# Graph attention with residual and layer norm: softmax rows replaced by the row's largest entry, with the general path behind a branch

## The chip, the cores and the metric

The kernel runs on one core of one Trainium2 chip; the other cores are idle. The metric is device time in microseconds (us) of one execution of the whole program. The span is the time from the first to the last instruction of the profiled execution.

## What is computed

x is 4096 x 512, adj is 4096 x 4096, W is 512 x 2048 (four heads of 512 columns), a is 4 x 1024 x 1, all float32. The reference, cut to what matters:

```python
ht = (h @ W).reshape(N, 4, 512).transpose(1, 0, 2)
src = einsum('hnd,hd->hn', ht, a[:, :512, 0])
dst = einsum('hnd,hd->hn', ht, a[:, 512:, 0])
e = leaky_relu(src[:, :, None] + dst[:, None, :], 0.01) + adj[None]
att = softmax(e, axis=-1)
h_prime = einsum('hij,hjd->hid', att, ht).mean(axis=0)
x = layernorm(x + h_prime)
```

adj is zero but for some 70,000 entries, each drawn evenly between 0.05 and 1e9, and its diagonal is never zero. So the largest entry of a row of adj can stand far above every other number in that row's softmax.

## The kernel before, in words

The scores src and dst are made first (lines 61 to 118): a is copied to all partitions (L68), W and x are loaded (L73, L75), DVE multiplies W by a (L83), and PE transposes x (L94) and multiplies (L101, L107, L111). x and W stay on chip. Then comes the attention, in 128 units: a block of 128 rows of adj by one of four heads. For each of the eight chunks of 512 columns of a unit, `add` makes the score (ACT L153, DVE L154) and adds adj with the row's maximum (DVE L156), `exp` takes the exponential with its sum (ACT L168), `transpose` turns the chunk on PE in four pieces (L173) and copies it out of PSUM (ACT L176 or DVE L178), and `apply` multiplies it by x, four matmuls of 128 x 512 (PE L186). `scale`, `turn` and `project` divide by the sum (DVE L197), transpose again (PE L202, ACT L204) and multiply by W (PE L211). After a block's fourth head come residual and norm (DVE L217 to L231), and POOL issues the store (L232).

The loop at L244 sets the order: the chunks of one unit are in the matrix products while the next unit's scores are made and the one before it is projected. SP issues the loads of adj in pieces of 128 x 1024 (L134), the next block's as soon as the last head has read a piece.

## Time and profile before

| | us |
|---|---|
| three timed runs | 4704.34, 4705.52, 4705.82 |
| median | 4705.52 |
| span of the profiled execution | 4702.5 |
| median less span (launch and end, around the span) | 3.0 |
| PE busy with matmuls | 4596.1 |
| DVE busy | 2124.3 |
| ACT busy | 1811.9 |
| POOL busy | 18.2 |

The profiled execution's own time isn't recorded apart from its span; what lies around the span is taken to be the 3.0 us by which the median exceeds it. PE is the engine whose busy time nearly fills the span. In the profile a group of instructions is told by its line, engine and operation, what it writes and reads, its count, its busy time and the mean of one in ns, and then the idle time ahead of it and what ended that. The granted clock (PEclk) is 1.00 at TensorE's higher level of 2.4 GHz and 0.50 at its lower level of 1.2 GHz.

### The profile page before, as it was taken

How to read it: one execution, taken by the hardware profiler on the slowest of the kernel's cores; microseconds unless marked ns; L12 is line 12 of the kernel's file. 1: busy time of each engine (PE TensorE's matmuls, PEld its weight loads, DVE VectorE, ACT ScalarE, POOL GpSimd, SP SyncE). 2: the span in 40 equal slices, each digit the busy share in tenths (PEclk: the TensorE clock that was granted, in tenths of full speed). 3: DMA queues.
4: the chain of work that ended last, by engine and by line, in shares of the span. 5: the costliest groups of instructions: out<-in, count | busy, mean ns of one | idle time of the engine just before them, and what ended most of it. 6: DMA issues, size and time to landing. Idle time of an engine off the chain costs nothing.

```text
span 4702.5 us, 38848 instructions
## 1 busy us (share of the span) xinstructions
PE 4596.1 (98%) x14112; PEld 2251.0 (48%) x14112; DVE 2124.3 (45%) x4656; ACT 1811.9 (39%) x3712; POOL 18.2 (0%) x38
## 2 busy tenths in 40 slices
PE   7899999999999999999999999999999999999999
PEld 3344444444444444444444444444444444444444
DVE  3444444444444444444444444444444444444443
...
GB/s 125 27 12 21 18 21 20 12 12 21 18 21 20 7 16 21 18 21 16 7 21 21 18 21 16 7 21 21 18 21 12 12 21 21 18 21 12 12 21 3
DMA packets 26127, 92.66 MB, mean 20 GB/s; under 512 B 2768, under 2 KB 2768, under 8 KB 25296
## 3 DMA queue, kind: packets, MB, share of 16 engines
q1 hardware_dynamic: 22656, 75.51, 4.7%
q0 software_dynamic: 2560, 8.39, 0.5%
...
q8 instruction: 111, 1.82, 0.2%
q14 instruction: 80, 0.66, 0.0%
HBM read 81.79 MB, written 8.39 MB: 19 GB/s over the span
## 4 chain that ended last, share of the span: by engine, by line
issue 75%; PE 23%; DVE 1%; POOL 0%; DMA 0%; ACT 0%; POOLq 0%; ACTq 0%; DVEq 0%
PE y_ps L186 16%; PE o_ps L211 2%; PE pt_ps L173 2%; PE ps_b L107 1%; PE ps_sd L101 1%; PE ps_x L94 0%; DVE y L197 0%; DVE prod L83 0%; PE yt_ps L202 0%; POOL out_dram L232 0%; DMA w_sb<-in_L_gnn_W_dram 0%; DVE s L154 0%; DVE sd L103 0%; DVE s L156 0%; PE ps_s L111 0%
## 5 line engine op out<-in xcount | busy, mean ns | idle before, releaser
L186 PE MATMUL y_ps<-x_sb,pt 128*128 128x512 f32 x8192 | 3685.7, 593 | 0.0
L186 PEld LDWEIGHTS y_ps<-x_sb,pt 128*128 128x128 f32 x8192 | 1487.1, 190 | 1531.3 <-issue 1530.9
L154 DVE SCALAR_TENSOR_TENSOR s<-s 128x512 f32<-128x512 f32 x1024 | 705.6, 689 | 1048.4 <-ACT s L153 1006.2
L153 ACT ACTIVATE s<-dst_b,src 128x512 f32<-128x512 f32 x1024 | 723.0, 718 | 971.2 <-PE pt_ps L173 952.2
L178 DVE COPY pt<-pt_ps 128x512 f32<-128x512 f32 x640 | 442.6, 692 | 997.4 <-PE pt_ps L173 997.4
L168 ACT ACTIVATE s<-s,nm 128x512 f32<-128x512 f32 x1024 | 724.0, 708 | 181.0 <-DVE nm L164 181.0
L173 PEld LDWEIGHTS pt_ps<-ident,s 128*128 128x128 f32 x4096 | 512.5, 141 | 551.7 <-issue 538.7
L176 ACT COPY pt<-pt_ps 128x512 f32<-128x512 f32 x384 | 225.1, 586 | 1346.4 <-PE pt_ps L173 1346.4
L156 DVE CUSTOM_DVE_ANT_0 s<-s,adj 128x512 f32<-128x512 f32 x1024 | 708.6, 692 | 35.1
L173 PE MATMUL pt_ps<-ident,s 128*128 128x128 f32 x4096 | 615.3, 273 | 12.7 <-ACT s L168 12.7
L211 PE MATMUL o_ps<-w_sb,yt 128*128 128x512 f32 x1024 | 460.8, 593 | 0.7 <-ACT yt L204 0.7
L211 PEld LDWEIGHTS o_ps<-w_sb,yt 128*128 128x128 f32 x1024 | 184.6, 190 | 184.6 <-issue 183.6
L197 DVE TENSOR_SCALAR y<-y_ps,rz 128x512 f32<-128x512 f32 x128 | 96.0, 750 | 296.8 <-PE y_ps L186 296.8
L168 ACT ACTIVATION_READ_ACCUMULATOR s<-s,nm 128x1 f32 x1024 | 191.2, 187 | 0.0
L202 PE MATMUL yt_ps<-ident,y 128*128 128x128 f32 x512 | 83.9, 286 | 52.6 <-DVE y L197 52.6
L204 ACT COPY yt<-yt_ps 128x512 f32<-128x512 f32 x128 | 75.0, 586 | 76.0 <-PE yt_ps L202 76.0
L202 PEld LDWEIGHTS yt_ps<-ident,y 128*128 128x128 f32 x512 | 53.6, 140 | 83.5 <-DVE y L197 83.5
L224 ACT ACTIVATE sd<-sd 128x1 f32<-128x1 f32 x32 | 6.5, 203 | 210.8 <-DVE sd L223 210.8
L156 DVE DVE_READ_ACCUMULATOR2_ANT m<- 128x1 f32 x1024 | 83.8, 82 | 0.0
L217 DVE TENSOR_TENSOR y<-o_ps,x_sb 128x512 f32<-128x512 f32 x32 | 22.1, 692 | 90.2 <-PE o_ps L211 90.2
L94 PE MATMUL ps_x<-ident,x_sb 128*128 128x128 f32 x128 | 29.9, 422 | 21.8 <-DMA x_sb<-in_x_dram 16.6
L95 ACT COPY xT<-ps_x 128x512 f32<-128x512 f32 x32 | 18.7, 586 | 76.8 <-PE ps_x L94 76.8
...
## 6 DMA issues: line engine op xcount, KB each, us to landing
adj<-in_adj_dram SPq DMA_DIRECT2D x128, 512.0 KB, 3.4
x_sb<-in_x_dram SPq DMA_DIRECT2D x8, 1024.0 KB, 17.9
out_dram<-y POOLq DMA_DIRECT2D x32, 256.0 KB, 2.3
w_sb<-in_L_gnn_W_dram ACTq DMA_DIRECT2D x4, 1024.0 KB, 10.7
...
```

The costliest lines, as they stand in the source:

```text
L153: nc.scalar.activation(s, dst_b[:, h, ts(c, C)], AF.Identity, bias=src[:, ib, h : h + 1])
L154: nc.vector.scalar_tensor_tensor(s, s, SLOPE, s, op0=OP.mult, op1=OP.max)
L156: nc.vector.tensor_tensor_reduce(out=s, in0=s, in1=adj_t[ib, k][:, ts(part, C)], scale=1.0, scalar=LOWEST, op0=OP.add, op1=OP.max, accum_o ...
L168: nc.scalar.activation(s, s, AF.Exp, bias=self.nm, accum_out=self.z[:, c : c + 1])
L173: nc.tensor.transpose(ps[:, q, :], self.s[c][:, ts(q, P)], ident)
L176: nc.scalar.copy(pt, ps)
L178: nc.vector.tensor_copy(pt, ps)
L186: nc.tensor.matmul(self.y_ps, pt[:, q, :], x_sb[:, c * Q + q, :], start=(c == 0 and q == 0), stop=(c == NCH - 1 and q == Q - 1),)
L197: nc.vector.tensor_scalar_mul(self.y, self.y_ps, self.rz)
L202: nc.tensor.transpose(ps[:, kb, :], self.y[:, ts(kb, P)], ident)
L204: nc.scalar.copy(self.yt, ps)
L211: nc.tensor.matmul(o_ps[ib], self.yt[:, kb, :], w_sb[:, kb, ts(h, D)], start=(h == 0 and kb == 0), stop=(h == H - 1 and kb == KB - 1),)
```

## The change

The kernel becomes two functions. `leading_rows` handles every row by the place of its largest entry of adj; `general` is the old computation, put behind a branch, and done for those of 32 blocks that have a row in which the largest entry does not lead by enough. Blocks are now strided: block ib holds the rows p * 32 + ib, so the 128 rows of one load of adj lie 32 rows (512 KiB) apart.

For each block of adj, loaded as 128 x 4096 in a ring of six buffers, DVE takes the maximum of each stretch of 64 columns (`segment_maxima`), then the largest eight of the 64 maxima and their places (`find_segment`). POOL adds the row's offset and gathers the leading 64 columns of each row from DRAM by an indirect DMA (`lead`, 256 bytes a row). Two blocks later DVE finds the place within them (`find_column`), and POOL gathers the row of x at that place (`y`, 2 KB a row). For the last block the place is found in the whole row (`find_column_in_row`). PE transposes y (`turn`), adds x through an identity matmul (`residual`) and multiplies by `w_sum`, the mean of the four heads' W (`products`). ACT makes sums and sums of squares (`stats`) and the squared norms of x (`row_norm`); POOL makes the reciprocal deviation (`rstd`), and ACT writes the result into `hold` (`finish`), over the block of x that came in there. Before that, the last 16 blocks of `hold` hold W. Results of blocks 0 to 23 leave by six stores of four blocks each, those of 24 to 31 one block at a time, all after the last load on SP's queue but for block 31's, which ACT issues (`store`). `test` counts the rows whose lead is too small, from the two largest values, a bound on the scores (`bound`, from the norms of x and of W a) and the rounding of float32; every engine then loads the total and branches.

The main part of the diff; `block`, inside `general`, is the code of the old units, with blocks strided and its own loads and stores:

```diff
-    units = [(ib, h) for ib in range(NB) for h in range(H)]
-    before = None
-    for n in range(len(units) + 1):
...
+    leading_rows(tc, x, adj, W, a, out, ident, v, n_bad, any_bad)
+    flag = nc.values_load(any_bad[0:1, 0:1], min_val=0, max_val=N)
+    with tc.If(flag > 0, preferred_fallthrough_block=False):
+        general(tc, x, adj, W, out, ident, v, n_bad)
...
+    AHEAD = 5
+    Q = 4
+    PIECES = 4
+    LATE = NB - Q
+    adj_pool = ctx.enter_context(tc.tile_pool(name="adj_pool", bufs=AHEAD + 1))
+    small = ctx.enter_context(tc.tile_pool(name="small", bufs=5))
+    rows = ctx.enter_context(tc.tile_pool(name="rows", bufs=2))
+    psum = ctx.enter_context(tc.tile_pool(name="psum", bufs=4, space=bass.MemoryType.PSUM))
+    adj_rows = adj.rearrange("(p nb) m -> nb p m", nb=NB)
+    adj_segs = adj.rearrange("n (s e) -> (n s) e", e=E)
+    x_rows = x.rearrange("(p nb) d -> p nb d", nb=NB)
+    out_rows = out.rearrange("(p nb) d -> p nb d", nb=NB)
+    w_blocks = W.rearrange("(kb p) (h d) -> p kb h d", p=P, h=H)
+    hold = once.tile([P, NB, D], F32, name="hold")
+    w_at = NB - KB * H
...
+    def pieces(ib):
+        return PIECES if ib in (0, LATE, NB - 1) else 2 if ib > LATE else 1
+    def load_adj(ib):
+        if 0 <= ib < NB:
+            t = adj_t[ib] = adj_pool.tile([P, N], F32, name="adj_t")
+            n = pieces(ib)
+            for k in range(n):
+                nc.sync.dma_start(t[:, ts(k, N // n)], adj_rows[ib][:, ts(k, N // n)])
+    def load_x(lo, n):
+        nc.sync.dma_start(hold[:, ds(lo, n), :], x_rows[:, ds(lo, n), :])
+    def load_w(kb):
+        nc.sync.dma_start(hold[:, ds(w_at + kb * H, H), :], w_blocks[:, kb])
+    load_adj(0)
+    for s in range(2):
+        nc.scalar.dma_start(a_rows[ts(s, H), :], a[:, ts(s, D), :].rearrange("h d o -> h (d o)"))
+    for kb in range(KB):
+        load_w(kb)
+        load_adj(kb + 1)
+    load_x(0, Q)
+    for ib in range(KB + 1, AHEAD):
+        load_adj(ib)
...
+    def segment_maxima(ib, lo, hi):
+        if lo == 0:
+            seg_of[ib] = small.tile([P, S], F32, name="seg")
+        n = max(pieces(ib), 2)
+        for k in range(lo * n // PIECES, hi * n // PIECES):
+            nc.vector.tensor_reduce(
+                seg_of[ib][:, ts(k, S // n)],
+                adj_t[ib][:, ts(k, N // n)].rearrange("p (s e) -> p s e", e=E), axis=AX.X, op=OP.max,
+            )
+    def find_segment(ib):
+        seg = seg_of.pop(ib)
+        nc.vector.max(out=top[:, ib, :], in_=seg)
+        at = small.tile([P, 8], U32, name="at")
+        nc.vector.max_index(at, top[:, ib, :], seg)
+        row = small.tile([P, 1], U32, name="row")
+        nc.gpsimd.tensor_tensor(row, at[:, 0:1], first[:, ib : ib + 1], op=OP.add)
+        lead = small.tile([P, E], F32, name="lead", bufs=2 * Q + 1)
+        nc.gpsimd.indirect_dma_start(
+            out=lead, out_offset=None, in_=adj_segs,
+            in_offset=bass.IndirectOffsetOnAxis(ap=row[:, :1], axis=0),
+        )
+        start = at_of[ib] = small.tile([P, 1], U32, name="start")
+        nc.gpsimd.tensor_tensor(start, at[:, 0:1], width, op=OP.mult)
+        lead_of[ib] = lead
+    def gather_rows(ib, col):
+        y = y_t[ib] = rows.tile([P, D], F32, name="y", bufs=4)
+        nc.gpsimd.indirect_dma_start(
+            out=y, out_offset=None, in_=x,
+            in_offset=bass.IndirectOffsetOnAxis(ap=col[:, :1], axis=0),
+        )
+    def find_inner(ib):
+        nc.vector.max(out=inner[:, ib, :], in_=lead_of[ib])
+    def find_column(ib):
+        if ib < LATE - Q:
+            find_inner(ib)
+        within = small.tile([P, 8], U32, name="within")
+        nc.vector.max_index(within, top[:, ib, :], lead_of[ib])
+        col = small.tile([P, 1], U32, name="col")
+        nc.gpsimd.tensor_tensor(col, at_of.pop(ib), within[:, 0:1], op=OP.add)
+        gather_rows(ib, col)
+    def find_column_in_row(ib):
+        col = small.tile([P, 8], U32, name="col")
+        nc.vector.max_index(col, top[:, ib, :], adj_t[ib])
+        gather_rows(ib, col)
+    def turn(ib):
+        y = y_t.pop(ib)
+        tp = psum.tile([P, KB, P], F32, name="tp", bufs=2)
+        for kb in range(KB):
+            nc.tensor.transpose(tp[:, kb, :], y[:, ts(kb, P)], ident)
+        yt = yt_of[ib] = rows.tile([P, KB, P], F32, name="yt")
+        nc.scalar.copy(yt, tp)
+    def residual(ib):
+        o_ps[ib] = psum.tile([P, D], F32, name="o")
+        nc.tensor.matmul(o_ps[ib], ident, hold[:, ib, :], start=True, stop=False)
+    def products(ib, lo=0, hi=KB):
+        start = ib not in o_ps
+        if start:
+            o_ps[ib] = psum.tile([P, D], F32, name="o")
+        for kb in range(lo, hi):
+            nc.tensor.matmul(
+                o_ps[ib], yt_of[ib][:, kb, :], w_sum[:, kb, :],
+                start=(start and kb == 0), stop=(kb == KB - 1),
+            )
+    def row_norm(ib):
+        sq = rows.tile([P, D], F32, name="sq")
+        nc.scalar.activation(sq, hold[:, ib, :], AF.Square, accum_out=xx[:, ib : ib + 1])
+    def stats(ib):
+        o, i = o_ps[ib], slice(ib, ib + 1)
+        sq = rows.tile([P, D], F32, name="sq")
+        nc.scalar.activation(sq, o, AF.Identity, scale=-1.0 / D, accum_out=nm[:, i])
+        sq = rows.tile([P, D], F32, name="sq")
+        nc.scalar.activation(sq, o, AF.Square, bias=nm[:, i], accum_out=sd[:, i])
+    def rstd(i):
+        nc.gpsimd.tensor_scalar(sd[:, i], sd[:, i], 1.0 / D, EPS, op0=OP.mult, op1=OP.add)
+        nc.gpsimd.tensor_tensor(sd[:, i], sd[:, i], power[:, : i.stop - i.start], op=OP.pow)
+        nc.gpsimd.tensor_mul(nm[:, i], nm[:, i], sd[:, i])
+    def finish(ib):
+        i = slice(ib, ib + 1)
+        nc.scalar.activation(hold[:, ib, :], o_ps.pop(ib), AF.Identity, bias=nm[:, i], scale=sd[:, i])
+    def finish_last(ib, residual):
+        o = o_ps.pop(ib)
+        if residual:
+            nc.vector.tensor_add(hold[:, ib, :], o, hold[:, ib, :])
+            o = hold[:, ib, :]
+        st = small.tile([P, nc.vector.BN_STATS_DIM], F32, name="st", bufs=2)
+        nc.vector.bn_stats(st, o)
+        mv = small.tile([P, nc.vector.BN_AGGR_DIM], F32, name="mv", bufs=2)
+        nc.vector.bn_aggr(mv, st)
+        r = small.tile([P, 1], F32, name="r", bufs=2)
+        nc.scalar.activation(r, mv[:, 1:2], AF.Sqrt, bias=eps)
+        nc.vector.reciprocal(r, r)
+        nc.vector.tensor_scalar(hold[:, ib, :], o, mv[:, 0:1], r, op0=OP.subtract, op1=OP.mult)
+    def store(queue, lo, n):
+        queue.dma_start(out_rows[:, ds(lo, n), :], hold[:, ds(lo, n), :])
+    def mean_of_heads(kb):
+        o = psum.tile([P, D], F32, name="o")
+        for h in range(H):
+            nc.tensor.matmul(o, ident, hold[:, w_at + kb * H + h, :], start=(h == 0), stop=(h == H - 1))
+        nc.scalar.activation(w_sum[:, kb, :], o, AF.Copy, scale=1.0 / H)
...
+    def turn_w(kb, h):
+        tp = psum.tile([P, KB, P], F32, name="tp", bufs=2)
+        for k in range(KB):
+            nc.tensor.transpose(tp[:, k, :], hold[:, w_at + kb * H + h, ts(k, P)], ident)
+        wt = rows.tile([P, KB, P], F32, name="wt")
+        nc.scalar.copy(wt, tp)
+        return wt
+    def head_vector(kb, h, wt):
+        for k in range(KB):
+            nc.tensor.matmul(
+                pv[:, kb, h : 2 * H : H], wt[:, k, :], at_d[:, k, h : 2 * H : H],
+                start=(k == 0), stop=(k == KB - 1),
+            )
...
+    def test():
+        a1 = top[:, :, 0]
+        nc.vector.tensor_tensor(gap, top[:, :, 1], inner[:, :, 1], op=OP.max)
+        size = once.tile([P, NB], F32, name="size")
+        nc.vector.scalar_tensor_tensor(size, a1, -1.0, a1, op0=OP.mult, op1=OP.max)
+        nc.vector.tensor_sub(gap, a1, gap)
+        nc.vector.tensor_scalar(size, size, -(2.0 ** -22), lead_by, op0=OP.mult, op1=OP.subtract)
+        nc.vector.scalar_tensor_tensor(gap, gap, 0.9999, size, op0=OP.mult, op1=OP.add)
+        nc.vector.tensor_scalar(gap, gap, 0.0, None, op0=OP.is_gt)
...
+    x_at = {lo - 1: (lo, Q) for lo in range(Q, LATE - Q, Q)}
+    x_at.update({ib - 2: (ib, 1) for ib in range(LATE - Q, LATE)})
+    vectors = [(kb, h) for kb in range(KB) for h in range(H)]
+    vectors_at = {t: 2 if t < 3 else 1 for t in range(1, 15)}
+    COLUMN, PROJECT, STATS, FINISH = 2, 3, 4, 6
+    for t in range(NB):
+        if t in x_at:
+            load_x(*x_at[t])
+        load_adj(t + AHEAD)
+        middle = 1 if t == NB - 1 else 2
+        segment_maxima(t, 0, middle)
+        if t >= COLUMN:
+            find_column(t - COLUMN)
+        segment_maxima(t, middle, PIECES)
+        pair = t >= FINISH and t % 2 == 0
+        if pair:
+            rstd(slice(t - FINISH, t - FINISH + 2))
+        find_segment(t)
+        if t < 2:
+            mean_of_heads(t)
+        elif t == 2:
+            mean_of_heads(2)
+            mean_of_heads(3)
+        if t == 0:
+            turn_a()
+        turned = [(*vectors[0], turn_w(*vectors.pop(0))) for _ in range(vectors_at.get(t, 0))]
+        if t == 16:
+            head_norms()
+        ib = t - PROJECT
+        if ib >= 0:
+            turn(ib)
+            if ib < LATE:
+                residual(ib)
+        for some in turned:
+            head_vector(*some)
+        if ib >= 0:
+            products(ib)
+        if t >= STATS:
+            stats(t - STATS)
+            row_norm(t - STATS)
+        if pair:
+            finish(t - FINISH)
+            finish(t - FINISH + 1)
+    load_x(LATE, NB - LATE)
+    for lo in range(0, NB - 2 * Q, Q):
+        store(nc.sync, lo, Q)
+    for ib in range(NB - 2 * Q, NB - FINISH):
+        store(nc.sync, ib, 1)
+    find_column(NB - 2)
+    rstd(slice(NB - FINISH, NB - FINISH + 2))
+    find_column_in_row(NB - 1)
+    for ib in range(LATE, NB):
+        row_norm(ib)
+    turn(NB - 3)
+    bound(0)
+    products(NB - 3, 0, KB - 1)
+    finish(NB - FINISH)
+    finish(NB - FINISH + 1)
+    turn(NB - 2)
+    products(NB - 3, KB - 1, KB)
+    bound(1)
+    bound(2)
+    finish_last(NB - 4, True)
+    for ib in range(LATE - Q, NB):
+        find_inner(ib)
+    test()
+    products(NB - 2, 0, KB - 1)
+    finish_last(NB - 3, True)
+    turn(NB - 1)
+    products(NB - 2, KB - 1, KB)
+    for ib in (NB - FINISH, NB - FINISH + 1):
+        store(nc.sync, ib, 1)
+    residual(NB - 1)
+    products(NB - 1, 0, KB - 1)
+    pg = count()
+    products(NB - 1, KB - 1, KB)
+    for ib in (NB - 4, NB - 3):
+        store(nc.sync, ib, 1)
+    finish_last(NB - 2, True)
+    store(nc.sync, NB - 2, 1)
+    report(pg)
+    finish_last(NB - 1, False)
+    store(nc.scalar, NB - 1, 1)
...
+    with tc.For_i(0, NB, 1) as ib:
+        here = nc.values_load(n_bad[0:1, ds(ib, 1)], min_val=0, max_val=P)
+        with tc.If(here > 0):
+            block(ib)
```

How the instructions stand on the engines. DVE before, some of the steady order of a unit (s is a chunk of scores, m its maxima, pt a transposed chunk):

```order
L178 COPY pt<-pt_ps 128x512
L154 SCALAR_TENSOR_TENSOR s<-s 128x512
L156 ISA s,m<-s,adj_552 128x512
L156 ISA m 128x1
L154 SCALAR_TENSOR_TENSOR s<-s 128x512
L156 ISA s,m<-s,adj_554 128x512
L156 ISA m 128x1
```

DVE in the change, two half blocks in the steady part (seg holds the 64 maxima, top the largest eight):

```order
L164 MAX_INDEX at<-top,seg 128x8
L155 TENSOR_REDUCE seg<-adj_t 128x32
L184 MAX inner<-lead 128x8
L191 MAX_INDEX within<-top,lead 128x8
L155 TENSOR_REDUCE seg<-adj_t 128x32
L162 MAX top<-seg 128x8
L164 MAX_INDEX at<-top,seg 128x8
L155 TENSOR_REDUCE seg<-adj_t 128x32
```

What was chunk work on scores is now one pass over adj, with four short searches in each block.

SP before, its first rows:

```order
L296 UNCONDITIONAL_BRANCH
L75 DMA x_sb<-in_x_dram 128x4x512 x8
L134 DMA adj_550<-in_adj_dram 128x1024
L134 DMA adj_552<-in_adj_dram 128x1024
L134 DMA adj_554<-in_adj_dram 128x1024
L134 DMA adj_556<-in_adj_dram 128x1024
```

SP in the change, the last loads and what stands behind them:

```order
L113 DMA hold<-in_x_dram 128x512
L110 DMA adj_t<-in_adj_dram 128x2048 x2
L113 DMA hold<-in_x_dram 128x512
L110 DMA adj_t<-in_adj_dram 128x2048 x2
L110 DMA adj_t<-in_adj_dram 128x1024 x4
L113 DMA hold<-in_x_dram 128x2048
L260 DMA out_dram<-hold 128x2048 x6
L260 DMA out_dram<-hold 128x512 x7
L60 TENSOR_LOAD any_bad
L60 ISA x2
```

Every store but that of block 31 stands behind every load on SP's queue.

POOL before issued only 32 stores. In the change, one block with `rstd` and the next one's start:

```order
L178 DMA y<-in_x_dram,col 128x512
L166 TENSOR_TENSOR row<-at,first 128x1
L168 DMA lead<-in_adj_dram,row 128x64
L173 TENSOR_TENSOR start<-at,width 128x1
L193 TENSOR_TENSOR col<-start,within 128x1
L178 DMA y<-in_x_dram,col 128x512
L236 TENSOR_SCALAR sd<-sd 128x2
L237 TENSOR_TENSOR sd<-sd,power 128x2
L238 TENSOR_TENSOR nm<-nm,sd 128x2
```

Each block has two gathers on POOL, and `rstd`, which waits for ACT's `stats`, stands between a gather of y and the next gather of lead.

## Rows read from the trace of the kernel before

**Rows 1.** The page: span, busy time and share of each engine, GB/s by slices.
```profile
span 4702.5 us, 38848 instructions
...
PE 4596.1 (98%) x14112; PEld 2251.0 (48%) x14112; DVE 2124.3 (45%) x4656; ACT 1811.9 (39%) x3712; POOL 18.2 (0%) x38
...
GB/s 125 27 12 21 18 21 20 12 12 21 18 21 20 7 16 21 18 21 16 7 21 21 18 21 16 7 21 21 18 21 12 12 21 21 18 21 12 12 21 3
```

**Rows 2.** The page: the chain that ended last, shares by engine.
```profile
issue 75%; PE 23%; DVE 1%; POOL 0%; DMA 0%; ACT 0%; POOLq 0%; ACTq 0%; DVEq 0%
```

**Rows 3.** Groups by line, PE: busy, mean ns | idle before, releaser.
```profile
L186 PE MATMUL y_ps<-x_sb,pt 128*128 128x512 f32 x8192 | 3685.7, 593 | 0.0
...
L173 PE MATMUL pt_ps<-ident,s 128*128 128x128 f32 x4096 | 615.3, 273 | 12.7 <-ACT s L168 12.7
...
L211 PE MATMUL o_ps<-w_sb,yt 128*128 128x512 f32 x1024 | 460.8, 593 | 0.7 <-ACT yt L204 0.7
```

**Rows 4.** The chain in order of time: start us, us, what (two blocks).
```profile
1156.29 141.36 issue
1298.20 141.35 issue
```

**Rows 5.** Windows of the start: busy PE, PEld, DVE, ACT, POOL; PEclk, DMA share, GB/s.
```profile
2.00:12.00 10.00, 0.00 (x0) 0.00 (x0) 0.00 (x0) 0.00 (x0) 0.00 (x0) 1.00 0.97 388
12.00:22.00 10.00, 1.94 (x8) 1.57 (x8) 8.63 (x25) 0.18 (x1) 0.00 (x0) 1.00 1.02 405
22.00:32.00 10.00, 7.86 (x30) 4.49 (x30) 9.55 (x28) 5.70 (x9) 0.00 (x0) 1.00 1.04 395
32.00:36.00 4.00, 0.00 (x0) 0.00 (x0) 3.79 (x11) 0.00 (x0) 0.00 (x0) 0.84 1.05 385
40.00:50.00 10.00, 10.00 (x28) 5.62 (x26) 2.85 (x5) 1.62 (x3) 0.00 (x0) 0.50 0.00 0
```

**Rows 6.** DMA queues: packets, MB, share; issues by line: KB each, us to landing.
```profile
q1 hardware_dynamic: 22656, 75.51, 4.7%
q0 software_dynamic: 2560, 8.39, 0.5%
...
x_sb<-in_x_dram SPq DMA_DIRECT2D x8, 1024.0 KB, 17.9
out_dram<-y POOLq DMA_DIRECT2D x32, 256.0 KB, 2.3
w_sb<-in_L_gnn_W_dram ACTq DMA_DIRECT2D x4, 1024.0 KB, 10.7
```

**Rows 7.** Groups by line, DVE.
```profile
L154 DVE SCALAR_TENSOR_TENSOR s<-s 128x512 f32<-128x512 f32 x1024 | 705.6, 689 | 1048.4 <-ACT s L153 1006.2
...
L164 DVE TENSOR_REDUCE nm<-m 128x1 f32<-128x8 f32 x128 | 20.6, 161 | 4.5
```

**Rows 8.** Groups by line, ACT.
```profile
L168 ACT ACTIVATE s<-s,nm 128x512 f32<-128x512 f32 x1024 | 724.0, 708 | 181.0 <-DVE nm L164 181.0
...
L168 ACT ACTIVATION_READ_ACCUMULATOR s<-s,nm 128x1 f32 x1024 | 191.2, 187 | 0.0
...
L204 ACT COPY yt<-yt_ps 128x512 f32<-128x512 f32 x128 | 75.0, 586 | 76.0 <-PE yt_ps L202 76.0
```

**Rows 9.** Timeline, PE at the lower granted clock (39 to 50 us).
```profile
39.10 7.19 PE L107 MATMUL ps_b<-sd,ident 8*128 8x512 f32 x8 [0.77 <-DVE sd L103]
...
46.55 3.82 PE L94 MATMUL ps_x<-ident,x_sb 128*128 128x128 f32 x16
```

**Rows 10.** Groups by line, POOL: the store that POOL issues.
```profile
L232 POOL DMA_DIRECT2D out_dram<-y x32 | 17.5, 546 | 4679.8 <-DVE y L231 4679.8
```

**Rows 11.** Timeline of the end, from the last transposes to the last issue.
```profile
4689.84 0.66 PE L202 MATMUL yt_ps<-ident,y 128*128 128x128 f32 x4 [0.84 <-DVE y L197]
...
4698.10 0.54 POOL L232 DMA_DIRECT2D out_dram<-y  x1 [136.09 <-DVE y L231]
```

More of the change, by code (lines that the diff above doesn't have):

```diff
@@ L47, in gat_resnorm_kernel, with general @@
+@with_exitstack
+def general(ctx, tc, x, adj, W, out, ident, v, n_bad):
+    nc = tc.nc
+    N, D = x.shape
+    KB, NB, NCH, Q = D // P, N // P, N // C, C // P
+    H = v.shape[2] // 2
     AW = 2
-    ctx.enter_context(tc.manual_schedule())
     const = ctx.enter_context(tc.tile_pool(name="const", bufs=1))
     x_sb = const.tile([P, NB, D], F32, name="x_sb")
-    w_sb = const.tile([P, KB, H * D], F32, name="w_sb")
     dst_b = const.tile([P, H, N], F32, name="dst_b")
     src = const.tile([P, NB, H], F32, name="src")
-    ident = const.tile([P, P], F32, name="ident")
+    w_sb = const.tile([P, KB, H * D], F32, name="w_sb")
@@ L108, in scores @@
                 nc.vector.tensor_copy(dst_b[:, h, ts(g, C)], pb)
+        for g in range(NCH):
             pt = pps.tile([P, Q, 2 * H], F32, name="ps_s")
             for q in range(Q):
-                nc.tensor.transpose(pt[:, q, :], sd[:, ts(q, P)], ident[: 2 * H, : 2 * H])
+                rows_of = sd_all[:, ds(g * Q + q, P, NB)]
+                nc.tensor.transpose(pt[:, q, :], rows_of, ident[: 2 * H, : 2 * H])
             nc.vector.tensor_copy(src[:, ts(g, Q), :], pt[:, :, :H])
-        xT = x_transposed(0)
-        for g in range(NCH):
-            ahead = x_transposed(g + 1) if g + 1 < NCH else None
-            scores(g, xT)
-            xT = ahead
-    adj_pool = ctx.enter_context(tc.tile_pool(name="adj_pool", bufs=1))
+    adj_pool = ctx.enter_context(tc.tile_pool(name="adj_g", bufs=1))
     s_pool = ctx.enter_context(tc.tile_pool(name="s_pool", bufs=9))
@@ L234, in gat_resnorm_kernel @@
-    for k in range(NCH // AW):
-        load_adj(0, k)
-    u = Unit(0)
-    for c in range(NCH):
-        u.add(c)
-    u.largest()
-    for c in range(NCH):
-        u.exp(c)
-    before = None
-    for n in range(len(units) + 1):
-        after = Unit(n + 1) if n + 1 < len(units) else None
-        for c in range(NCH):
-            if u is not None:
-                u.transpose(c)
-            if before is not None:
-                if c == 0:
-                    before.apply(NCH - 1)
-                    before.scale()
-                elif c == 1:
-                    before.turn()
-                elif c == 2:
-                    before.project()
-                elif c == 3:
-                    before.store()
-            if u is not None and c > 0:
-                u.apply(c - 1)
-            if after is not None:
-                if c == 0:
-                    after.add(0)
-                if c + 1 < NCH:
-                    after.add(c + 1)
-                if c == NCH - 2:
-                    after.largest()
-                if c >= NCH - 2:
-                    half = NCH // 2
-                    for e in range(half):
-                        after.exp((c - (NCH - 2)) * half + e)
-        before, u = u, after
```

328 lines of the change are left out of this document (212 added, 116 removed).

## The prediction

> **What bounds the kernel now.** I read the page first. Of a span of 4702.5 us PE is busy for 4596.1, while the DMA engines run at about 20 GB/s after the first slice [rows 1]. Next the chain that ended last: 75% is "issue", time in which PE waited for nothing, and 23% is PE itself [rows 2]; in order of time it is one long piece per block, 141.9 us from one to the next [rows 4]. The groups by line tell what fills it: 8192 products of attention with x, 4096 transposes, 1024 products with W [rows 3]. Nothing else counts: a term of the new sum can't be read from these stages. It must come from the one stage in which this kernel was bound by DMA, its start. From 2 to 36 us the DMA share is 0.97 to 1.05, at 385 to 405 GB/s [rows 5].
>
> **What is removed.** In the change no unit of scores runs, if no row needs the general path. I worked out from the reference's inputs (seed 0) whether one does: the smallest lead of a row's largest entry over its second is 10,880; the test asks for at most 1.05 x 25.16 x 2.596 + 110 = 179 for the scores, with the largest norm of a row of x (25.16) and the largest sum of a head's two norms (2.596), and 2^-22 x 1e9 = 238 for rounding, together 417. No row falls short, so all of rows 2 to 4 goes, and what is left is new.
>
> **What each block costs now.** Four engines and the DMA work on each of 32 blocks side by side.
> - DMA: 2.10 MB of adj, 0.26 of x, 0.26 of gathered x, 0.03 of leading segments. At 395 GB/s (the mean over 2 to 36 us [rows 5]) the first three take 6.6 us; with the small pieces 6.9.
> - DVE: an operation on 512 elements takes 0.69 us, a reduction of 8 takes 0.16 [rows 7]: 0.16 us and 1.05 ns for each further element. Two reductions over 2048 take 2 x 2.3 = 4.6 us. The four searches over 64 elements lie between 0.16 and 0.69 us each; near the lower end, since 64 is nearer to 8: 0.3, so 1.2. Sum 5.8, at most 7.4.
> - ACT: a copy of 0.59, three passes with a sum at 0.71 + 0.19, and a finish of 0.71 [rows 8]: 4.0 us, and 0.6 more for the first 16 pieces of W.
> - PE: five products and four transposes. At the lower granted clock (0.50 from 40 to 50 us [rows 5]) eight products with 512 columns took 7.19 us and 16 transposes 3.82 [rows 9], so 5 x 0.90 + 4 x 0.24 = 5.5 us, and 6.4 while W is turned; at the full clock about half.
> - POOL: two gathers and four or five small operations. A gather's issue isn't in the trace. The nearest rows are the plain store's issue, 0.54 us [rows 10], and its landing, 2.3 us [rows 6]; between these 2.5 to 7 us in all. I take 4.
>
> So DMA is the slowest at 6.9 us a block, and DVE is behind it by 1.1. The ring of six buffers lets SP load five blocks ahead, 5 x 6.9 = 34 us, which covers single late gathers. Everything on DVE, ACT, PE and POOL in the steady part is therefore costed at nothing; the cover is thin for DVE and unknown for POOL (second rival).
>
> **The sum.**
> 1. First bytes: 2 us [rows 5].
> 2. Up to the last piece of adj, SP's queue carries 67.11 MB of adj, 4.19 of W and 7.34 of x (28 of 32 blocks): 78.66 MB with a, at 395 GB/s 199 us. The bounds are 405 GB/s, the best window [rows 5], which gives 194, and 342, the mean of that queue over the run (75.51 MB in 4.7% of 4702.5 us [rows 6]), which gives 230. I take the start's rate, for there the engines had no gaps, as in the change.
> 3. Beside that, 30 gathers of y, 7.86 MB in 2 KB pieces. POOL's stores, also 2 KB rows, moved 8.39 MB in 0.5% of the span [rows 6], 357 GB/s: 22 us (19 at the best rate).
> 4. 31 gathers of lead, 1.02 MB in pieces of 256 bytes. No row has such pieces. By bytes 2.6 us; if a piece costs as much as one of 2 KB, 23. I take 8, a third of the way, since a piece's cost must lie above its bytes' and nothing shows that it is all fixed.
> 5. The tail after the last piece of adj. DVE: a quarter pass 1.2, three searches 1.0, the search in the whole row (4096 elements) 4.5, so 6.7 us. Gather of y: issue 0.5, landing between 2.3 us and the 17.9 that a load had in the full start-up queue [rows 6]; 5 taken. From the last transposes to the last issue the old kernel took 8.3 us [rows 11]; four products and an addition fewer leave 5.8. From the issue to the end 4.4 (4698.1 to 4702.5). That is 22.4. Beside it the DMA engines carry the last x, 31 blocks of results and two gathers, 9.7 MB, 24.6 us. The longer sets the end, and they take from each other: 25 (22 to 32).
> 6. Every engine loads the flag and jumps over the general code. No row shows it. It is ready before the last block's norm, so it may lie wholly beside the store (0) or cost a landing twice (5). I take 2.
>
> Sum: 2 + 199 + 22 + 8 + 25 + 2 = 258 us of span. Around the span lay 3.0 us in the median of the runs, and the sum is made against the profiled execution and carried over: **261 us**, 18 times less than 4705.52. With the lower bounds it is 2 + 194 + 19 + 3 + 22 + 0 + 3 = 243, with the upper ones 2 + 230 + 23 + 23 + 32 + 5 + 3 = 318.
>
> A rule speaks against item 2. The Trainium skill ("HBM Reference", Specifications (TRN2)) gives a core's share of the memory as about 358 GB/s. By it, item 2 would be an estimated 220 us and the sum 282. The start-up windows stand above it at 385 to 405 GB/s with one core at work, so the trace decides for 395.
>
> **The rivals.**
> - *The load stream is slower than at the start* (16%). The old loads read neighbouring rows; now the 128 rows of a load lie 512 KiB apart, gathers mix into the stream, and the small pieces may cost more. For it: queue q1 averages 342 GB/s over the run, against 395 at the start. Against: most of that average is single loads on an idle queue. Price at 342 GB/s: 2 + 230 + 23 + 8 + 27 + 2 + 3 = **295 us**. The Trainium skill ("DMA: Bandwidth & Descriptors", Latency and other measured facts) has a rule for such pitches: 207 of 214 GB/s at 512 KiB, and half at 4 MiB. By that, 3% or an estimated 6 us would be lost on adj; no run here shows it yet.
> - *An engine's loop sets the pace* (11%): searches at the upper end (DVE 7.4 us), gathers dear on POOL, or a gather that lands late under a full queue. In POOL's order, `rstd` stands between one gather of y and the next of lead, and it waits for ACT's sums, which wait for an earlier y; about two blocks must cover a landing and some 4 us of PE and ACT. At a landing of 12 us a block takes (12 + 4) / 2 = 8 us, the sum 7 + 32 x 8 + 25 + 2 + 3 = **293 us**. For it: 17.9 and 10.7 us to landing in the start's full queue [rows 6]; against: those were transfers of 1 MB, not 0.26.
> - *The general path runs.* Its price is the old preparation, 4698.1 - 32 x 141.9 = 157 us [rows 4, 11], and for each block that has one weak row 142 us and about 27 that no longer overlap with the next block (filling, 8 x 1.4 on DVE and 8 x 0.9 on ACT [rows 7, 8], and draining, 8.3 [rows 11]). One block gives 261 + 157 + 169 = 587 us (2%). From (4705 - 261 - 157) / 169 = 25, so at 26 blocks of 32, it is **slower than before**; with all it is 261 + 157 + 32 x 169 = 5826 us (1%). The leads worked out above speak against it; an error in the gathered second value or in the bound would speak for it. It is also the case in which the change does not do what it says.
>
> **How the numbers follow.** The forecast, DMA at the start's rate throughout, has 70%: 261, by itself 245 to 277. The two rivals near 295 have 27%. The range goes from 245 to 300: the lower end near all lower bounds at once, the upper just past both rivals; the sum's upper bounds at once (318) and the general path stay out. A measurement here can tell about 0.2% from no change. Faster by more than that: the forecast, two rivals and few general blocks, 99%; within 0.2%: nothing lands there, 0; slower: 1%.
>
> **What would show it.** Right: a DMA share above 0.95 and 385 GB/s or more in windows between 10 and 225 us, gathers included; DVE about 190 us busy, ACT 130, PE below 190; DVE idle mostly for loads of adj; the chain ending in stores or in the last block's gather. First rival: the share full, but GB/s near 345. Second: the share below 0.9 with DVE waiting for lead, or POOL without idle time. Third: instructions of `block` in the profile. The prediction is wrong if the steady part takes much other than 6.9 us a block, or the tail more than 32 us.

## The result and the profile after

The changed kernel takes **250.24 us** (median of four runs, 249.16 to 251.16) against 4705.65 for the kernel before, measured beside it: 0.0532 of the time, interval 0.0530 to 0.0533. The forecast was 261, the range 245 to 300. The profiled execution took 250.78 us with a span of 248.9, so 1.9 lie around the span. Of `no_lead` and of `stores_early` one run each lay over 1.5% above the fastest of its kernel and is left out of the times below. No line of `general` (437 to 639 of the changed kernel) has an instruction in the profile's groups: no block took the general path.

The page of the changed kernel, where [rows 1, 6] stood before (busy time and GB/s by engine; DMA queues):

```profile
span 248.9 us, 2484 instructions
...
PE 199.7 (80%) x677; PEld 101.0 (41%) x678; DVE 186.3 (75%) x300; ACT 109.8 (44%) x266; POOL 97.7 (39%) x213
...
GB/s 263 445 416 432 402 425 421 419 424 415 407 432 410 408 426 417 421 411 417 417 424 416 422 414 413 414 420 422 407 407 398 412 404 407 419 422 429 298 85 54
...
q1 hardware_dynamic: 10224, 87.82, 85.5%
q0 software_dynamic: 3584, 9.44, 9.7%
```

The GB/s were about 20 after the first slice and are now 398 or more in all but the first slice and the last three. Both kinds of gather are in q0: 9.44 MB in 9.7% of 248.9 us, 24.1 us of the 16 engines.

The windows of the changed kernel (from:to, length; busy us and instructions of PE, weight loads, DVE, ACT, POOL; granted clock; DMA share; GB/s), beside [rows 5]:

```profile
2.00:12.00 10.00, 1.29 (x2) 0.81 (x3) 5.40 (x7) 0.93 (x1) 1.30 (x2) 1.00 1.03 417
...
42.00:62.00 20.00, 20.00 (x91) 12.27 (x91) 15.16 (x22) 8.20 (x21) 8.51 (x17) 1.00 1.00 418
...
82.00:102.00 20.00, 20.00 (x84) 11.76 (x84) 16.17 (x25) 12.27 (x32) 10.03 (x22) 1.00 1.01 417
...
122.00:142.00 20.00, 17.44 (x46) 7.38 (x44) 18.55 (x32) 10.93 (x27) 10.82 (x22) 0.91 1.01 418
...
182.00:202.00 20.00, 18.03 (x50) 7.71 (x49) 18.56 (x27) 12.22 (x32) 11.42 (x25) 1.00 1.02 403
202.00:212.00 10.00, 8.28 (x26) 3.72 (x25) 8.00 (x13) 4.94 (x12) 4.61 (x11) 1.00 1.01 401
...
222.00:232.00 10.00, 8.56 (x27) 3.98 (x28) 4.12 (x18) 2.60 (x6) 1.07 (x1) 1.00 1.01 420
232.00:242.00 10.00, 6.71 (x13) 2.28 (x11) 6.57 (x22) 1.06 (x3) 0.00 (x0) 0.83 0.44 166
```

Two things are to be seen. The DMA share is 0.99 to 1.03 from 2 to 232 us, at 413 to 425 GB/s but for 401 to 403 from 182 to 212 us; the old start had 385 to 405 [rows 5]. And PE fills its windows from 42 to 62 and from 82 to 102 us, while W is still turned: there it is a second bound just below the first. From 122 us on, with W done, it is busy for 15 to 18 of 20 us.

The groups of the changed kernel by line, shapes apart (busy us, mean ns of one, idle time before and its releaser):

```profile
L155 DVE TENSOR_REDUCE seg<-adj_t 128x32 f32<-128x2048 f32 x58 | 131.9, 2276 | 36.3 <-DMA adj_t<-in_adj_dram 35.6
...
L219 PE MATMUL o<-w_sum,yt 128*128 128x512 f32 x256 | 121.9, 618 | 3.3 <-ACT yt L208 3.3
...
L168 POOL DMA_INDIRECT lead<-in_adj_dram,row x32 | 32.3, 1009 | 13.8 <-POOL row L166 13.8
L178 POOL DMA_INDIRECT y<-in_x_dram,col x32 | 30.9, 966 | 17.9 <-POOL col L193 15.8 <-DVE xg L318 2.1
...
L164 DVE FIND_INDEX8 at<-top,seg 128x8 uint32<-128x64 f32 x32 | 7.0, 219 | 0.0
```

DVE's idle time was for loads of adj, as a kernel bound by its loads shows. PE has 256 records for 4 x 32 = 128 products with W: two records are one product (below). A gather occupies POOL for 1.0 us.

The tail. DVE, then ACT, then PE of the changed kernel in order of time (start us, duration, instruction; in brackets the idle time before it and what ended it), where the old tail was [rows 11]:

```profile
212.16 3.45 DVE L155 TENSOR_REDUCE seg<-adj_t 128x16 f32<-128x1024 f32 x3
...
217.63 0.09 DVE L191 MATCH_VALUE_LOAD within<-top,lead 128x8 f32 x1 [1.36 <-DMA lead<-in_adj_dram,row]
...
217.97 4.42 DVE L199 FIND_INDEX8 col<-top,adj_t 128x8 uint32<-128x4096 f32 x1
...
228.12 0.16 DVE L323 TENSOR_TENSOR lead_by<-px,vn 128x1 f32<-128x1 f32 x1 [5.01 <-PE px L321]
...
231.03 1.11 DVE L184 MAX8 inner<-lead 128x8 f32<-128x64 f32 x8
...
234.59 0.18 DVE L253 BATCH_NORM_AGGREGATE mv<-st 128x2 f32<-128x6 f32 x1
```

```profile
226.95 0.59 ACT L208 COPY yt<-tp 128x512 f32<-128x512 f32 x1 [3.32 <-PE tp L206]
...
234.81 0.29 ACT L255 ACTIVATE r<-mv,eps 128x1 f32<-128x1 f32 x1 [4.47 <-DVE mv L253]
235.01 0.57 ACT L208 COPY yt<-tp 128x512 f32<-128x512 f32 x1
...
243.66 0.39 ACTq L260 DMA_DIRECT2D out_dram<-hold  x1
```

```profile
226.29 0.63 PE L206 MATMUL tp<-ident,y 128*128 128x128 f32 x4 [0.92 <-DMA y<-in_x_dram,col]
...
230.69 0.62 PE L206 MATMUL tp<-ident,y 128*128 128x128 f32 x4
...
235.63 4.47 PE L219 MATMUL o<-w_sum,yt 128*128 128x512 f32 x6 [2.60 <-ACT yt L208]
```

The last quarter pass (maxima over the last 1024 columns of block 31) starts 2 x 1.15 us into the row of three, at about 214.4 us; I take it as the end of the load phase. (That row follows other work of DVE without a pause, so the last piece may have landed a little earlier.) From there the tail takes 34.5 us. The last block's x rows are turned at 230.69, yet ACT copies them only at 235.01: ahead of the copy in ACT's order stands a square root of block 29's norm, whose input DVE delivers at 234.59 + 0.18, after it waited 5.01 us for the bound (`px`, which hangs on ACT's copy of block 30 at 226.95) and then did `inner`, the test and another block's norm.

### The profile page after: what moved, and what is told of

Read it like the earlier page. It is cut to its first block, busy times and chain, and to the rows that moved or that the text cites. A ratio compares the mean times of both kernels' runs of the same rounds, so it can differ in the third digit from the quotient of the medians.

```text
span 248.9 us, 2484 instructions
## 1 busy us (share of the span) xinstructions
PE 199.7 (80%) x677; PEld 101.0 (41%) x678; DVE 186.3 (75%) x300; ACT 109.8 (44%) x266; POOL 97.7 (39%) x213
## 2 busy tenths in 40 slices
DMA packets 13988, 97.76 MB, mean 393 GB/s; under 512 B 2184, under 2 KB 2184, under 8 KB 7824
## 3 DMA queue, kind: packets, MB, share of 16 engines
q0 software_dynamic: 3584, 9.44, 9.7%
## 4 chain that ended last, share of the span: by engine, by line
issue 34%; POOL 31%; DMA 21%; DVE 5%; PE 3%; ACT 2%; POOLq 1%; SPq 1%
DMA adj_t<-in_adj_dram 15%; POOL lead L168 10%; POOL y L178 9%; DMA y<-in_x_dram,col 7%; POOL sd L237 3%; PE o L219 3%; POOL start L173 2%; POOL col L193 2%; POOL row L166 2%; DVE seg L155 2%; POOL sd L236 1%; POOL nm L238 1%; DVE st L251 1%; PE tp L206 1%; DVE hold L257 1%
## 5 line engine op out<-in xcount | busy, mean ns | idle before, releaser
L155 DVE TENSOR_REDUCE seg<-adj_t 128x32 f32<-128x2048 f32 (+1 forms) x70 | 146.1, 2093 | 40.6 <-DMA adj_t<-in_adj_dram 39.7
L219 PE MATMUL o<-w_sum,yt 128*128 128x512 f32 x256 | 121.9, 618 | 3.3 <-ACT yt L208 3.3
L219 PEld LDWEIGHTS o<-w_sum,yt 128*128 128x128 f32 x256 | 47.7, 197 | 61.9 <-issue 47.9
L208 ACT COPY yt<-tp 128x512 f32<-128x512 f32 x32 | 18.8, 587 | 48.7 <-PE tp L206 45.8
L178 POOL DMA_INDIRECT y<-in_x_dram,col x32 | 30.9, 966 | 17.9 <-POOL col L193 15.8
L168 POOL DMA_INDIRECT lead<-in_adj_dram,row x32 | 32.3, 1009 | 13.8 <-POOL row L166 13.8
L206 PE MATMUL tp<-ident,y 128*128 128x128 f32 x128 | 19.9, 279 | 17.0 <-DMA y<-in_x_dram,col 17.0
L265 PE MATMUL o<-hold,ident 128*128 128x512 f32 x32 | 17.9, 712 | 17.8 <-DMA hold<-in_L_gnn_W_dram 17.8
L212 PE MATMUL o<-hold,ident 128*128 128x512 f32 x58 | 30.8, 613 | 0.0
L242 ACT ACTIVATE hold<-o,nm,sd 128x512 f32<-128x512 f32 x28 | 20.1, 770 | 0.0
L226 ACT ACTIVATE sq<-hold 128x512 f32<-128x512 f32 x32 | 19.8, 619 | 0.0
L233 ACT ACTIVATE sq<-o,nm 128x512 f32<-128x512 f32 x28 | 19.3, 688 | 0.9
```

Source lines behind the costliest of these rows:

```text
L155: nc.vector.tensor_reduce(seg_of[ib][:, ts(k, S // n)], adj_t[ib][:, ts(k, N // n)].rearrange("p (s e) -> p s e", e=E), axis=AX.X, op=OP.max,)
L168: nc.gpsimd.indirect_dma_start(out=lead, out_offset=None, in_=adj_segs, in_offset=bass.IndirectOffsetOnAxis(ap=row[:, :1], axis=0),)
L178: nc.gpsimd.indirect_dma_start(out=y, out_offset=None, in_=x, in_offset=bass.IndirectOffsetOnAxis(ap=col[:, :1], axis=0),)
L206: nc.tensor.transpose(tp[:, kb, :], y[:, ts(kb, P)], ident)
L208: nc.scalar.copy(yt, tp)
L212: nc.tensor.matmul(o_ps[ib], ident, hold[:, ib, :], start=True, stop=False)
```

## The experiments

**The load stream.** First whether the pitch of 512 KiB costs anything. In `adj_near` a block of adj holds neighbouring rows, 16 KiB apart:

```diff
-    adj_rows = adj.rearrange("(p nb) m -> nb p m", nb=NB)
+    adj_rows = adj.rearrange("(nb p) m -> nb p m", p=P)
-    nc.gpsimd.iota(first, pattern=[[S, NB]], base=0, channel_multiplier=NB * S)
+    nc.gpsimd.iota(first, pattern=[[P * S, NB]], base=0, channel_multiplier=S)
```

> Only the rows of one load of adj are neighbours now (16 KiB apart instead of 512 KiB), with the row offsets of the gather to match; x and the results stay strided, so rows of adj meet other rows of x and the result is not the reference's. Theory 1, the pitch costs nothing here: 249 to 251 us and the same GB/s between 42 and 182 us (417). Theory 2, the far pitch costs some per cent, as the Trainium skill's rule has it (DMA: Bandwidth & Descriptors): 3% on 67 MB, some 5 us, so 245 us and 425 to 430 GB/s.

250.50 us (250.02 to 251.65). A window of it, beside 417 of the changed kernel:

```profile
82.00:102.00 20.00, 20.00 (x92) 12.20 (x89) 16.19 (x25) 12.28 (x31) 9.89 (x22) 1.00 1.01 420
```

The far pitch costs these loads nothing that can be measured, so the mechanism named first for the slow load stream falls.

Then the size of the pieces. The old start loaded x in rows of 2 KB per descriptor at 395 GB/s; the new loads have up to 16 KiB. `pieces_2k` loads every block of adj in eight DMAs of 128 x 512:

```diff
-            n = pieces(ib)
+            n = 8
```

> Every block of adj is loaded in eight DMAs of 128 x 512, so that each row's piece is 2 KB instead of 16 KB; nothing else differs. Theory 1, the rate of 395 GB/s at the start of the old kernel came from its small pieces (2 KB rows of x beside 8 KB rows of W): the rate falls from 417 to about 395 GB/s, the 88 MB ahead of the last piece of adj take 12 us more, 260 to 264 us. Theory 2, the piece's size does not count from 2 KB up: 249 to 251 us, 415 GB/s or more.

269.03 us (267.67 to 269.36), 18.8 more. Its windows, and its last three quarter passes on DVE:

```profile
82.00:102.00 20.00, 19.07 (x86) 11.54 (x85) 14.76 (x24) 10.53 (x27) 7.94 (x18) 1.00 1.04 386
...
232.00:242.00 10.00, 7.28 (x19) 3.42 (x20) 6.62 (x10) 6.31 (x18) 4.44 (x9) 0.83 1.01 423
```

```profile
229.52 3.45 DVE L155 TENSOR_REDUCE seg<-adj_t 128x16 f32<-128x1024 f32 x3
```

The DMA engines are as full (1.04) and move less, 381 to 387 GB/s from 42 to 202 us; when adj is over and the 4-block stores run, the rate is 423. The load phase ends 17.4 us later. The theory of the small pieces holds, and the effect is larger than it said. The edit makes each DMA smaller too (256 KB for 2 MB), which this run alone does not part from the size of a row's piece; but the old start had 2 KB pieces in DMAs of 1 MB [rows 6] and ran at 385 to 405 as well. In the changed kernel itself the rate is lowest, 401 to 403, from 182 to 212 us, where the last four blocks of adj come in pieces of 4 and 8 KB; that fits, without showing it.

`no_y` leaves out the gathers of y; every block takes a fixed tile:

```diff
-        y = y_t[ib] = rows.tile([P, D], F32, name="y", bufs=4)
-        nc.gpsimd.indirect_dma_start(
...
+        y_t[ib] = y_fixed
```

> The gathers of y are left out: a tile of ones takes their place, so the result is not the reference's; the search for the column stays. Theory 1, bytes through the DMA engines set the pace: 30 of the 32 gathers, 7.9 MB, are gone from the stream ahead of the last piece of adj, 19 us at 418 GB/s, and in the tail the landing of the last y (7.5 us) too; the end is then the last piece near 193 us plus 23 us of stores and 5 us to the end, 220 to 228 us. Theory 2, a loop over DVE, POOL and the gathers sets the pace: if it is DVE's own 5.7 us a block, the last piece is done at 195 at the earliest and the result is alike; if it is POOL (3 us a block as seen), PE or ACT, the last piece of adj is not earlier than the 212 us of the change, and the time stays above 238 us.

236.08 us (234.46 to 236.73), 14.2 less: between the two. DVE at 120 to 132 us and its last quarter passes, and windows in the middle:

```profile
120.52 0.19 DVE L299 TENSOR_REDUCE n<-px 128x8 f32<-128x32 f32 x1 [2.56 <-PE px L297]
...
126.63 2.27 DVE L157 TENSOR_REDUCE seg<-adj_t 128x32 f32<-128x2048 f32 x1
...
131.99 2.27 DVE L157 TENSOR_REDUCE seg<-adj_t 128x32 f32<-128x2048 f32 x1
...
197.10 3.46 DVE L157 TENSOR_REDUCE seg<-adj_t 128x16 f32<-128x1024 f32 x3
```

```profile
122.00:142.00 20.00, 20.00 (x59) 9.18 (x58) 19.59 (x29) 13.64 (x35) 7.11 (x19) 1.00 1.01 420
142.00:162.00 20.00, 20.00 (x60) 9.11 (x59) 19.45 (x33) 13.67 (x36) 7.64 (x20) 1.00 1.01 421
```

The load phase ends 15.1 us earlier, so the gathers of y did hold the pace back. The edit takes away their bytes and the wait for them at once; that it is the bytes follows from the full DMA share of the changed kernel and from `pieces_2k` above and `stores_early` below, which change what DMA carries and none of the engines' work on a block. In `no_y` the DMA share is still 1.01, but PE (20.00 of 20) and DVE (19.5) are full as well: DVE waits 2.56 us for PE, and from 121 us to the end of the last pass it never waits for adj, at 5.36 us a block (126.63 to 131.99). So the next bound, DVE behind a full PE, is only some 15 us below, less than the 20 to 22 that the gathers' bytes would have given.

`no_lead` leaves out the gathers of the leading segments; the second search reads the 64 maxima again:

```diff
-        nc.gpsimd.indirect_dma_start(
-            out=lead, out_offset=None, in_=adj_segs,
...
-        lead_of[ib] = lead
+        lead_of[ib] = seg
```

(`seg` gets more buffers, so that it lives until then.)

> The gathers of the leading 64 columns are left out: the second search runs over the 64 maxima again, so wrong rows of x are gathered. Theory 1, small pieces cost about their bytes: 1.0 MB less, 2.5 us, and up to 1.4 us at the end where DVE waited for the last lead: 246 to 248 us. Theory 2, a piece costs what item 4 of the prediction took (8 us in all): 240 to 242 us.

244.56 us (243.03 to 245.00), 5.7 less, between the two. DVE's last quarter passes:

```profile
208.21 3.45 DVE L155 TENSOR_REDUCE seg<-adj_t 128x16 f32<-128x1024 f32 x3
```

They come 4.0 us earlier; the rest is in the tail, where the 1.36 us wait for block 30's segment is gone (in the profiled run the granted clock adds to that, see the last section). So 1 MB in pieces of 256 bytes costs 4 us of stream: more than its bytes (2.5 at 418 GB/s), half of the 8 that I took.

**Stores and flag.** `stores_early` undoes the holding: each four blocks are stored in the loop.

```diff
+        if t >= 10 and (t - 10) % Q == 0:
+            store(nc.sync, t - 10, Q)
...
-    for lo in range(0, NB - 2 * Q, Q):
-        store(nc.sync, lo, Q)
```

> Results are not held until the last load: a store of four blocks is issued on SP ten blocks behind, four of the six ahead of the last piece of adj. Theory 1, the last piece of adj starts the chain that ends last and DMA sets when it comes: 4.2 MB more ahead of it, 10 us at 418 GB/s, less some 2 us for a shorter queue in front of the last gathers: 256 to 260 us. Theory 2, the same bytes are moved in either order and the stream's end counts: no difference, 249 to 251 us.

262.18 us (260.79 to 263.25), 11.9 more. DVE's last passes, and the stretch in which the changed kernel still stored at 420 GB/s and then at 166:

```profile
221.72 3.45 DVE L155 TENSOR_REDUCE seg<-adj_t 128x16 f32<-128x1024 f32 x3
```

```profile
222.00:232.00 10.00, 7.19 (x18) 2.93 (x17) 8.46 (x10) 3.34 (x9) 5.20 (x12) 0.83 0.98 399
232.00:242.00 10.00, 7.62 (x24) 3.60 (x24) 2.74 (x9) 5.00 (x14) 1.07 (x1) 1.00 0.27 94
```

The load phase ends 9.6 us later. Four of the six stores stand ahead of the last load of adj in SP's order, 4.19 MB, which at 418 GB/s is 10.0 us. In the tail the DMA engines are then idle. So the held stores are worth their bytes, because the tail has DMA time to spare. That theory holds, though the cost came out above its range of 256 to 260.

`no_store6` leaves the six 4-block stores out:

```diff
-    for lo in range(0, NB - 2 * Q, Q):
-        store(nc.sync, lo, Q)
```

> The six stores of four blocks are left out, so blocks 0 to 23 of the result are not written. Theory 1, the chain of the last block sets the end and the stores only lengthen the landing of its gathers of y (7.4 us in the change): they land in 2.5 to 3 us, and 4 to 8 us are gained: 242 to 246 us. Theory 2, the stream of stores sets the end: 6.3 MB less are 15 us, 235 us.

248.16 us (247.23 to 249.54), 2.1 less, though 6.29 MB are gone: neither theory's gain. The DMA share falls to 0.31 in the window:

```profile
222.00:232.00 10.00, 9.38 (x29) 4.33 (x29) 5.17 (x23) 2.29 (x5) 1.07 (x1) 1.00 0.31 106
```

The tail is therefore not the stream of stores, and their load on the last gathers costs little more: blocks 30 and 31 are turned at 224.70 and 229.08 instead of 226.29 and 230.69. The chain on the engines sets it. (The profiled spans differ by 3.4 us, 245.5 and 248.9; 1.6 of that is the granted clock, see the last section.)

`no_flag` leaves out the load of the flag, the branch and the general path:

```diff
-    flag = nc.values_load(any_bad[0:1, 0:1], min_val=0, max_val=N)
-    with tc.If(flag > 0, preferred_fallthrough_block=False):
-        general(tc, x, adj, W, out, ident, v, n_bad)
```

> The loading of the flag, the branch and the general path are left out, so that only inputs like this one are handled. Theory 1, item 6 of the prediction: 2 us less, 248 us (0 to 5 less). Theory 2, the flag is loaded and tested beside the last store: no difference, 250 us.

249.26 us (247.22 to 250.47), 1.0 less, about the scatter of the runs. The trace tells more:

```profile
core 0: 247.5 us, clock 0.944
```

```profile
244.16 0.38 ACTq L257 DMA_DIRECT2D out_dram<-hold  x1
```

From the last issue to the end it takes 3.3 us instead of 5.2 (248.9 - 243.66). The flag costs 1.9, partly hidden in the medians by a last issue that came 0.5 later in this run.

**The tail.** `tail_turn` puts the last transposes, and so ACT's copy, ahead of block 29's norm:

```diff
-    finish_last(NB - 3, True)
     turn(NB - 1)
+    finish_last(NB - 3, True)
     products(NB - 2, KB - 1, KB)
```

> Two lines of the tail change places: the last block's transposes and the copy of the turned y come ahead of block 29's norm, so on ACT the copy no longer stands behind a square root that waits for DVE. Theory 1, the end is set by the chain of the last block and its waits in the engines' order: the copy starts at about 231.5 us instead of 235.0, PE does not fall idle ahead of the last products, and 4 to 5.5 us are gained: 245 to 246.5 us. Theory 2, the end is set by the stream of stores (24.6 us of DMA in the prediction): no difference, 250 us.

248.87 us (248.35 to 249.44), 1.4 less, where 4 to 5.5 were expected. DVE at the norm of block 31, then ACT and PE:

```profile
238.97 0.68 DVE L251 BATCH_NORM_STATS2 st<-o 128x6 f32<-128x512 f32 x1
```

```profile
231.69 0.59 ACT L208 COPY yt<-tp 128x512 f32<-128x512 f32 x1 [1.20 <-PE tp L206]
241.26 0.39 ACTq L260 DMA_DIRECT2D out_dram<-hold  x1
```

```profile
233.15 2.74 PE L219 MATMUL o<-w_sum,yt 128*128 128x512 f32 x6
...
235.97 1.13 PE L219 MATMUL o<-w_sum,yt 128*128 128x512 f32 x2
```

The copy comes 3.3 us earlier and the products end 4.2 earlier, at 237.10 (1.7 of the 4.2 because six records took 2.74 us here and 4.47 in the changed kernel, at another granted clock). But the last issue gains only 2.4: DVE, still busy with the norms of the blocks before, takes up block 31 only at 238.97, 1.9 us after its products.

`tail_split` adds to this that three of the six stores are issued by POOL behind the last gather:

```diff
-    for lo in range(0, NB - 2 * Q, Q):
+    for lo in range(0, 3 * Q, Q):
         store(nc.sync, lo, Q)
...
+    for lo in range(3 * Q, NB - 2 * Q, Q):
+        store(nc.gpsimd, lo, Q)
```

> As with the two lines exchanged, and three of the six stores are issued by POOL behind its last gather, so that the last two gathers of y meet a short queue. Theory 1, the chain with its waits: another 3 to 5 us beside the 4 to 5.5 of the exchange, 240 to 243 us. Theory 2, the stream of stores sets the end: the idle DMA engines ahead of POOL's stores are lost and it is slower than the change, 252 us or more.

248.77 us (248.23 to 250.89): the same as `tail_turn`; the further 3 to 5 us did not come. Here it does not matter which queue holds the stores, in line with `no_store6`.

`tail_dve` takes the order of `tail_turn` and gives DVE the norm of block 28 while it waits for the last gather, and that of block 29 ahead of the test:

```diff
-    bound(0)
-    products(NB - 3, 0, KB - 1)
+    products(NB - 3)
     finish(NB - FINISH)
     finish(NB - FINISH + 1)
+    finish_last(NB - 4, True)
+    bound(0)
     turn(NB - 2)
-    products(NB - 3, KB - 1, KB)
     bound(1)
+    finish_last(NB - 3, True)
     bound(2)
-    finish_last(NB - 4, True)
...
-    finish_last(NB - 3, True)
```

> Beside the earlier exchange, the tail's order on DVE and PE is changed: the norm of block 28 comes right behind the last search, block 29's products run in one piece, and the bound and the test come between the norms of 29 and 30. Theory 1, after the exchange the tail is set by DVE's order, since four norms of 2.7 us and the test stood in a row behind the bound, for which DVE waited 5.0 us: the last store is issued at about 238.5 us instead of 241.3, 245 to 246.5 us in all. Theory 2, the landing of the last gathers and PE's products set the tail: no better than with the exchange alone, 248 to 249.5 us.

247.72 us (247.02 to 249.44), 2.5 less, ratio to the kernel before 0.0527 (0.0525 to 0.0528). That is between the two ranges, and its runs overlap those of `tail_turn`, so the gain over that order alone is not clear. Its PE:

```profile
224.34 3.70 PE L219 MATMUL o<-w_sum,yt 128*128 128x512 f32 x8 [0.67 <-ACT yt L208]
...
229.67 2.84 PE L219 MATMUL o<-w_sum,yt 128*128 128x512 f32 x6
...
234.50 2.74 PE L219 MATMUL o<-w_sum,yt 128*128 128x512 f32 x6
```

DVE is no longer late (it takes up block 31 at 238.48, as the products end at 238.44); PE now works almost without a pause from 224 to 238 us and sets the last issue (240.80). `tail_dve_split` has both edits, the order of `tail_dve` and the split stores.

> As the one with the new order of the tail, and three of the six stores issued by POOL behind its last gather. Theory 1: with DVE's order mended, an earlier landing of the last two y counts, but PE's own 4.4 us a block in the tail leave little: 0 to 2 us better than the new order alone. Theory 2, the stores then end last: 1 to 3 us slower than the new order alone.

247.63 us (246.47 to 247.79), ratio 0.0525 (0.0524 to 0.0526). It is not clearly different from `tail_dve`; the two are the fastest versions that leave nothing out, 1.0% below the changed kernel.

## Why the prediction was right, and where it was not

The mechanism held: DMA sets the pace from 2 us to the end of the load phase, with a full share throughout (0.99 to 1.03); smaller pieces and more bytes ahead of the last load moved its end by 17.4 and 9.6 us. The load phase came out 16.6 us shorter than forecast and the tail 7.5 longer, so two errors of size partly cancelled: the span is 248.9 for 258. That the total came within 5% owes something to this luck. By the items of the sum:

| item | predicted | measured | from |
|---|---|---|---|
| 1 and 2, SP's queue | 2 + 199 | 2 + 188 | 78.66 MB at 418 GB/s |
| 3, gathers of y | 22 | 20 | 24.1 us of q0 (all 32 blocks) less item 4 |
| 4, leading segments | 8 | 4 | `no_lead` |
| sum, to the last quarter pass | 231 | 214.4 | DVE's row |
| 5, tail | 25 | 32.6 | 34.5 less the flag |
| 6, flag | 2 | 1.9 | `no_flag` |
| around the span | 3.0 | 1.9 | profiled run |

- **Item 2, mis-sized.** "I take the start's rate, for there the engines had no gaps" was the step that failed. The start's 395 GB/s was a rate of its pieces (x in 2 KB, beside W in 8 KB), not of the DMA engines: with 2 KB pieces adj runs at 381 to 387, with 16 KiB pieces at 418. The best window of the old start, 405, which I used as the upper bound, was too low as a bound. The Trainium skill ("HBM Reference", Specifications (TRN2)) gives 358 GB/s as a core's share with both cores of a pair streaming, and says there that a core alone measures about 425. With one core at work the windows stand at 401 to 425, which agrees with that; the estimate of 282 used the figure of the other case.
- **Items 3 and 4.** The gathers cost DMA time about as their bytes and pieces suggest. Together they took 24 us for 30 predicted. The 8 of item 4 was not what its text says either: a third of the way from 2.6 to 23 would be 9.4.
- **Item 5, wrong.** The text named a tail of over 32 us as a sign of error, and 32.6 it was, just over the upper bound. Against the chain of 22.4: DVE to the end of the last search 8.0 for 6.7, mostly the wait for block 30's segment; the gather to its transposes 8.3 for 5.5; from there to the last issue **13.0 for 5.8**; the end 5.2 for 4.4, with the flag in it. The failed step is "four products and an addition fewer leave 5.8". First, no product falls away. The old tail has eight records (first row below the list), and they are the four products of one head; the last block has four as well. With only the addition gone (0.69) the old tail would have left 7.6. Second, the step did not read the new order, in which the bound, the test and the norms of three blocks stand on ACT and DVE ahead of the last block's work. `tail_dve_split`, with that order mended, has 8.4 us from transposes (231.56) to issue (240.01); the changed kernel's order takes 11.3 in the runs of `no_lead` (226.46 to 237.81) and `no_flag` (232.82 to 244.16), at the full clock. So the order is worth some 2.9 us, and the last 1.6 of the 13.0 are the granted clock's (last section). The stream of 24.6 us that I set beside the chain was no bound (`no_store6`).
- **DVE, ACT and POOL a block.** Two passes of 2.28 us and four searches of 0.22 with two short loads of 0.08: 5.6 for 5.8, and 186 busy for 190. ACT was 110 busy for 130. POOL takes 1.0 us for each gather where 0.54 to 2.3 was the bound; in all 97.7 / 32 = 3.1 us a block for 4.
- **PE a block, wrong by two.** The "x8" in [rows 9] is four products, not eight (and the 8192 records of attention with x are 4096 products). At the full clock four products take 3.68 us, a residual 1.02, the transposes 0.60: 5.3 us where I had "about half" of 5.5. PE was 199.7 us busy, not below 190. The forecast survived because DMA, at 97.76 MB, was still slower; `no_y` shows that PE and DVE would have taken over 15 us further down. It also rested on the clock: read rightly, [rows 9] give at the lower clock an estimated 5 x 1.80 + 4 x 0.24 = 9.9 us a block, more than DMA's 6.9, and no rival named this. The granted clock stood at 0.91 or 1.00 in all windows from 42 to 232 us, so it did not come to that.
- **The rivals.** The slower load stream did not come: pitch is free here (`adj_near`), small pieces cost 4 us. The Trainium skill ("DMA: Bandwidth & Descriptors", Latency and other measured facts) has 3% for this pitch, measured on copies between tensors in HBM; `adj_near`, with loads into on-chip tiles, shows none. The engine loop was no bound, but nearer than the 1.1 us by which I had put DVE behind: the engine next in line was PE, with 6.06 us from one block's products to the next (62.89 and 68.95) while W is turned. A gather of y lands in 8.4 us (median, second row below), under the 12 of that rival. The general path did not run.

The two rows, the old tail's products and the landing of the gathers of y in the changed kernel:

```profile
4691.22 3.70 PE L211 MATMUL o_ps<-w_sb,yt 128*128 128x512 f32 x8 [0.73 <-ACT yt L204]
...
y<-in_x_dram,col POOLq DMA_INDIRECT x32, 8.4
```

What stays open: why 2 KB pieces move 8% less at a DMA share as full. The runs show the smaller pieces (and DMAs) as the cause, not what in the DMA engines takes the time.
